# Work beside the second attention: dealt by two engines' budgets, with layernorm arithmetic moved from VectorE to GpSimd

## The chip, the cores and the metric

The kernel runs on one core of one Trainium2 chip. The core has five engines that run their own instruction queues side by side: TensorE (PE in the profile; its weight loads are PEld), VectorE (DVE), ScalarE (ACT), GpSimd (POOL) and SyncE (SP, which only issues DMAs). The metric is the device time of one execution in microseconds; lower is better. Before the change it is 1583.2 us, the median of three runs (1580.79 to 1584.08).

## The reference

The input is `x` of shape (4, 1024, 256) in f32. Four layers run one after the other, each as `x = x + layernorm(layer(layernorm(x)))`:

```
x = x + _layernorm(_L0_attn_ref(_layernorm(x), ...))   # grouped attention, groups of 64
x = x + _layernorm(_L0_ffn_ref(_layernorm(x), ...))    # low-rank feed-forward
x = x + _layernorm(_L1_attn_ref(_layernorm(x), ...))   # the second attention
x = x + _layernorm(_L1_ffn_ref(_layernorm(x), ...))    # 8 experts, each takes its top 1024 tokens
```

The change lies in the third. It has 16 heads of 16 dimensions over 1024 tokens, in each of 4 rows of the batch:

```
qkv = (x @ w_qkv).reshape(Bx, Sx, H, 3 * HD); q, k, v = split(qkv)
scores = einsum('bhqd,bhkd->bhqk', q, k) / sqrt(HD)
w = relu(scores);  attn = w / (sum(w, -1) + 1e-6)
out = einsum('bhqk,bhkd->bhqd', attn, v) @ w_out + b_out
y = x + out
return (y - mu) * rsqrt(var + eps) * gamma + beta
```

Here `x` is the layernormed input. The result is layernormed once more and added to the residual. The rows for the experts are the layernorm of that sum.

## The kernel before

Tokens are held as 8 tiles `xs[t]` of 512 tokens, each `[128, 4, 256]`. The two first layers run as one pipeline over these 8 tiles, then comes the second attention, then the experts.

**Blocks and steps.** The second attention loops over the 4 rows `b`, the 2 halves of queries `qh` of a row, the 4 groups of heads `g` and the 8 tiles of keys `kt`. I call one `(b, qh)` a block (numbered 0 to 7) and one `kt` a step: a block has 32 steps, a group 8. The last block goes through its queries in two halves of 256 with two key tiles a step, so that it has 32 steps too, and 4 steps a group. A step does the following.

- `scores` (L1388): TensorE makes the scores of 4 heads. Two go to PSUM tiles called `sc1`, two to a double tile `sc2`. ScalarE takes the relu of the first two into `w` (L1397, two instructions), VectorE that of the other two in one instruction of 1024 columns (L1402). In the last block, ScalarE takes that pair in every second step (L1400).
- `finish` of the step before (`weigh`, L1414): TensorE multiplies `w` by the values with a column of ones, accumulating over `kt` in one PSUM bank `po`. After the last `kt` of a group VectorE transposes `po` into `turned` (L1464), and the next group's first multiplication has to wait for that, since it writes the same bank.
- One piece of TensorE's side work from the list `beside`, and some of VectorE's and ScalarE's side work from the list `rest`.

Everything stands in each engine's queue in the order in which it is written (`manual_schedule` for PE, DVE and ACT); the queues of POOL and SP are ordered by the framework's scheduler. So an instruction that waits holds up whatever stands behind it on its engine. PSUM gives three buffers to the `sc1` tiles and TensorE's side pieces together, two to `sc2`; `w` has two buffers.

**Side work.** In blocks 0 to 5 the queries, keys and values of the next row are made, one half-row a block: `normalize` (layernorm of `xs`, statistics and `apply`), then `project`: two pieces that transpose `h` (`turn`, L392), two each for queries, keys (L400) and values (L433). Queries and keys are split into a high and a low part: ScalarE writes the high one (L408, L419), VectorE the low one (L409, L420), both into a tile `parts` with two buffers, and SP stores them to DRAM (`q_d`, `k_d`), from where GpSimd's queue fetches them for the next row (`fetch_queries` L377, `fetch_keys` L370). In blocks 1 to 7 the block before is closed (`close`): two pieces `project_out` (L1201), then for each of the 4 tiles of 128 tokens the chain `stats_y`, `affine`, statistics of that, `shift`, `add`, `stats_x`, `token_rows_and_on`; the last stores the rows for the experts, and appends TensorE's pieces for the gate (`tpg` L1265, `pg` L1280). `divide` normalizes the heads of two groups by their sums.

Statistics (`scale_of`) are `bn_stats`, `bn_aggr` and an addition of eps on VectorE, then `(var+eps)^-0.5` on GpSimd (L1116).

**Dealing.** `by_tile` lists a chain as all tiles' first step, then all tiles' second, and so on. `go_on` takes in each step one piece of `beside` and with it two of `rest`, without one it takes one of `rest`; after the last `kt` of a group it takes a piece of `beside` alone:

```
def go_on(room=1):
    if beside:
        beside.pop(0)()
        room *= 2
    for _ in range(room):
        if rest:
            rest.pop(0)()
```

The last block deals by a time for VectorE instead (`go_on_for`). After the last step what is left is done, then `at_once` closes the last two tiles by itself.

Of the kernel before, what the change touches and what calls it, by code (L numbers as in the profile page):

```python
# [14 lines left out]
ALU = mybir.AluOpType  # L15
# [59 lines left out]
def kernel(  # L75
# [146 lines left out]
    with ExitStack() as st1:  # L222
# [127 lines left out]

        def open_row(hs=None):

            row = {"h": hs or [act4("h") for _ in range(BPB)]}
# [736 lines left out]
    with ExitStack() as st3:  # L1090
# [16 lines left out]
        def scale_of(tag, src):  # L1107

            st = small.tile([P, 6], F32, tag=f"st{tag}", name=f"st{tag}")
            mv = small.tile([P, 2], F32, tag=f"mv{tag}", name=f"mv{tag}")  # L1110
            ve = small.tile([P, 1], F32, tag=f"ve{tag}", name=f"ve{tag}")
            rs = small.tile([P, 1], F32, tag=f"rs{tag}", name=f"rs{tag}")
            nc.vector.bn_stats(st, src)
            nc.vector.bn_aggr(mv, st)
            nc.vector.tensor_scalar(ve, mv[:, 1:2], EPS, None, ALU.add)  # L1115
            nc.gpsimd.tensor_tensor(rs, ve, mhalf[:, 0:1], ALU.pow)  # L1116
            return mv[:, 0:1], rs


        VECTOR_US = {"affine": 0.9, "shift": 0.43, "add": 0.42, "token_rows_and_on": 0.35}  # L1120

        def by_tile(*steps, tiles=range(NJ)):

            kept = {}

            def run(do, i):
                kept[i] = do(i, *kept.get(i, ())) or ()

            def piece(do, i):
                def go():  # L1130
                    run(do, i)

                go.us = VECTOR_US.get(do.__name__, 0.65)
                return go

            return [piece(do, i) for do in steps for i in tiles]

        def normalize(row, b, k):

            h, x = row["h"][k], xs[b * BPB + k]  # L1140

            def stats(i):
                return scale_of("a", x[:, i, :])

            def apply(i, mean, rs):
                nc.vector.tensor_scalar(h[:, i, :], x[:, i, :], mean, rs, ALU.subtract, ALU.mult)

            return by_tile(stats, apply)
# [20 lines left out]
        def divide(state, t):  # L1169
# [20 lines left out]

            by_weight.us, back.us = (0.7, 0.45) if n < TB else (1.3, 0.75)
            return [by_weight, back]

        def close(t, h, oT, tiles, at_end):
# [25 lines left out]

            def affine(i, mean, rs):
                nc.vector.scalar_tensor_tensor(y[:, i, :], y[:, i, :], mean, gam, ALU.subtract, ALU.mult)
                nc.vector.scalar_tensor_tensor(y[:, i, :], y[:, i, :], rs, bet, ALU.mult, ALU.add)

            def shift(i, mean, rs):
                ms = small.tile([P, 1], F32, tag="msc", name="msc")
                nc.vector.scalar_tensor_tensor(ms, mean, -1.0, rs, ALU.mult, ALU.mult)
                x = xs[t][:, i, :]
                nc.scalar.activation(x, x, AF.Identity, bias=ms)
                return (rs,)  # L1230
# [7 lines left out]

            def token_rows(i, mean, rs):
                if t < ADDED:  # L1240
                    nc.sync.dma_start(out_flat[t][:, i, :], xs[t][:, i, :])
                if i == tiles[0]:
                    gating["h"] = wk.tile([P, NJ, D], F32, tag="hg", name="hg")
                hg = gating["h"][:, i, :]
                nc.vector.tensor_scalar(hg, xs[t][:, i, :], mean, rs, ALU.subtract, ALU.mult)
                nc.sync.dma_start(tok_d[t * TB + i * P : t * TB + (i + 1) * P, 0:D], hg)
                if i == tiles[-1]:
                    js = slice(tiles[0], tiles[-1] + 1)
                    rows = x_d[t * TB : (t + 1) * TB, :].rearrange("(j p) d -> p j d", p=P)
                    nc.sync.dma_start(rows[:, js, :], xs[t][:, js, :])  # L1250

            def token_rows_and_on(i, mean, rs):
                token_rows(i, mean, rs)
                if i % 2:
# [52 lines left out]
            def at_once(by_weight, back):  # L1307
# [39 lines left out]
                for i, mean, rs in moments("g", x, "take"):  # L1347
                    token_rows(i, mean, rs)
                turn_gating(tiles[0])
# [26 lines left out]
        def scores(row, qh, q2, halves, g, kt):  # L1376
# [19 lines left out]
            for j, sc in enumerate(singles):  # L1396
                nc.scalar.activation(w[:, j, :], sc, AF.Relu)  # L1397
            if halves > 1 and kt // halves % 2:

# [26 lines left out]

        def go_on(room=1):
            if beside:
                beside.pop(0)()
                room *= 2  # L1430
            for _ in range(room):
                if rest:
                    rest.pop(0)()

        spare_time = [0.0]

        def go_on_for(us, weights_on_act):

            left = min(spare_time[0], 0.3) + us
            if beside:  # L1440
                beside.pop(0)()
                left -= 0.45
            while rest:

                takes = 0.8 if weights_on_act and rest[0].us == VECTOR_US["shift"] else rest[0].us
                if takes > left:
                    break
                left -= takes
                rest.pop(0)()
            spare_time[0] = left  # L1450

# [27 lines left out]
        for b in range(B):  # L1479
            after = open_row() if b + 1 < B else None  # L1480
            for qh in range(BPB):
# [3 lines left out]
                if after is not None:  # L1485
# [4 lines left out]

                    and_project.us = last.us
                    rest.extend((*steps, and_project))
                halves = 2 if (b, qh) == (B - 1, BPB - 1) else 1
                for q2 in range(halves):
                    for g in range(NG):
                        for kt in range(0, KT, halves):
                            w = scores(row, qh, q2, halves, g, kt)
                            if before is not None:
                                finish(*before)
                            if kt == halves and g % 2 == 0:  # L1500
# [5 lines left out]
                            at_end = kt == KT - halves  # L1506
                            if halves == 1:
                                go_on(0 if at_end else 1)
                            elif kt // halves % 2:
                                go_on_for(1.5 if at_end else 1.8, True)  # L1510
# [569 lines left out]
```

## Time and profile before

| | us |
|---|---|
| median of 3 runs | 1583.2 |
| the profiled execution | 1582.82 |
| its span | 1581.0 |
| second attention, first scores to the end of the last block | 419.5 to 1045 |
| experts after it, to the end | 1045 to 1581 |

Of the profiled execution 1.8 us lie outside the span. Busy shares over the span are TensorE 95%, VectorE 61%, ScalarE 41%, GpSimd 27%; these are means over four different stages. The mean granted TensorE clock is 0.979. A matmul's end is modelled in the trace, so that a busy TensorE can still be waiting: the starts of the instructions tell more than their lengths.

The starts of the scores give each block's time (from the timeline, first scores of a block to the first scores of the next; block 7 to the start of its last step):

| block | 0 | 1 | 2 | 3 | 4 | 5 | 6 | 7 (31 steps) |
|---|---|---|---|---|---|---|---|---|
| us | 80.4 | 79.7 | 79.1 | 83.3 | 79.3 | 81.7 | 66.5 | 71.3 |

### The profile page before, as it was taken

Reading aid. Unit: us, or ns where it says so; the run is one execution under the profiler, and the core shown is the slowest. Engines: PE = TensorE matmul, PEld = TensorE weight load, DVE = VectorE, ACT = ScalarE, POOL = GpSimd, SP = SyncE. Lnnn points to the kernel's source line nnn. Section 1 sums busy time; section 2 is a strip of 40 time slices with the busy share of each in tenths; the row PEclk is TensorE's granted clock in tenths of the full one; section 3 lists DMA queues with packets and bytes.
Section 4 is the critical chain, followed back from the end, with each engine's and each line's share of the span. In section 5 each row is a group of like instructions: output and inputs, shape, how many; then the busy total and the mean of one; then the engine's idle time right before and its main releaser. Section 6 shows DMA issues by size and latency. Waiting matters only on the chain. (4 is left out here: it accounts for less than half of the span.)

```text
span 1581.0 us, 24173 instructions
## 1 busy us (share of the span) xinstructions
PE 1498.6 (95%) x9286; PEld 797.3 (50%) x9286; DVE 966.5 (61%) x2266; ACT 642.8 (41%) x1117; POOL 425.5 (27%) x473
## 2 busy tenths in 40 slices
PE   8999999999699899999999999977999999999996
PEld 4666666666333333333323323534665666676674
DVE  5555665565457887878787897776463732222145
ACT  4344445543345454545454556752112112211232
POOL 4122323322210212021212111112424332342554
PEclk9999999999899999999999999988999999999998
DMA  8300000004322323223232401042224233243364
GB/s 212 123 1 1 0 1 1 1 1 149 118 90 71 107 95 108 94 85 117 94 101 74 135 28 55 28 122 70 68 50 101 64 72 74 49 96 70 71 155 125
DMA packets 91886, 121.59 MB, mean 77 GB/s; under 512 B 24925, under 2 KB 64250, under 8 KB 91642
## 3 DMA queue, kind: packets, MB, share of 16 engines
q1 hardware_dynamic: 70000, 73.09, 14.6%
q0 software_dynamic: 21712, 46.94, 12.9%
q8 instruction: 73, 1.20, 0.3%
q14 instruction: 43, 0.35, 0.1%
q10 hardware_dynamic: 58, 0.01, 0.0%
HBM read 66.90 MB, written 53.12 MB: 76 GB/s over the span
## 5 line engine op out<-in xcount | busy, mean ns | idle before, releaser
L1397 ACT ACTIVATE w<-sc 128x512 f32<-128x512 f32 x512 | 277.7, 595 | 166.5 <-ACT w L1397 63.2
L1402 DVE TENSOR_SCALAR w<-sc 128x1024 f32<-128x1024 f32 x240 | 292.8, 1220 | 52.6 <-PE sc L1388 32.2
L1414 PE MATMUL po<-w,vaug 128*17 128x512 f32 (+1 forms) x2304 | 301.9, 553 | 10.4 <-DVE turned L1464 8.5
L1955 PE MATMUL ph<-xT,w 128*128 128x512 f32 (+1 forms) x544 | 229.7, 575 | 0.3 <-DVE xT L1938 0.3
L1972 PE MATMUL py<-w,hid 128*128 128x256 f32 x1024 | 229.7, 381 | 0.0
L1962 ACT ACTIVATE hid<-ph,mb 128x512 f32<-128x512 f32 (+1 forms) x136 | 90.0, 662 | 340.0 <-PE ph L1955 249.6
L1972 PEld LDWEIGHTS py<-w,hid 128*128 128x128 f32 x1024 | 192.0, 190 | 31.4 <-issue 6.7
L1388 PE MATMUL sc<-q,kT 32*128 32x512 f32 (+1 forms) x2304 | 195.8, 416 | 9.9 <-ACT w L1397 8.5
L1388 PEld LDWEIGHTS sc<-q,kT 32*128 32x128 f32 x2304 | 88.6, 185 | 184.2 <-issue 157.3
L1955 PEld LDWEIGHTS ph<-xT,w 128*128 128x128 f32 x544 | 100.0, 190 | 106.9 <-issue 98.2
L1993 POOL DMA_INDIRECT acc_d<-y,idx x56 | 88.1, 1573 | 227.5 <-DVE y L1992 104.4
L1414 PEld LDWEIGHTS po<-w,vaug 128*17 128x17 f32 x2304 | 50.1, 96 | 127.1 <-issue 73.3
L1991 DVE TENSOR_TENSOR y<-py,mb 128x256 f32<-128x256 f32 x56 | 23.5, 419 | 126.3 <-PE py L1972 116.8
L1763 POOL DMA_INDIRECT got<-tok_d,idx x64 | 66.3, 1036 | 61.3 <-DVE counts L1597 24.4
L1938 DVE COPY xT<-tp 128x512 f32<-128x512 f32 (+1 forms) x34 | 22.2, 658 | 71.4 <-PE tp L1933 65.2
L716 PE MATMUL pg<-nT,wh 128*128 128x512 f32 x128 | 61.6, 614 | 1.5 <-ACT nT L655 1.4
L838 PE MATMUL py<-wo,oT 128*128 128x256 f32 x256 | 61.9, 385 | 0.0
L732 PE MATMUL pv<-wh,nT 128*128 128x512 f32 x128 | 59.7, 593 | 0.0
L1116 POOL TENSOR_TENSOR rsg<-veg,mhalf 128x1 f32<-128x1 f32 x30 | 16.7, 556 | 148.3 <-DVE veg L1115 148.3
L838 PEld LDWEIGHTS py<-wo,oT 128*128 128x128 f32 x256 | 47.3, 190 | 17.1 <-issue 9.6
L903 ACT ACTIVATE hid<-ph,vec 128x512 f32<-128x512 f32 x64 | 39.8, 685 | 27.3 <-PE ph L894 27.1
L588 POOL TENSOR_TENSOR x<-x,y 128x1024 f32<-128x1024 f32 x14 | 32.9, 2354 | 59.9 <-ACT y L577 59.8
(298 smaller groups left out, 1995.0 us busy)
## 6 DMA issues: line engine op xcount, KB each, us to landing
q<-q_d POOLq DMA_DIRECT2D x16, 1024.0 KB, 6.3
w<-in_L_ffn_W_dram SPq DMA_DIRECT2D x16, 1024.0 KB
q_d<-parts SPq DMA_DIRECT2D x48, 256.0 KB
kT<-k_d POOLq DMA_DIRECT2D x16, 512.0 KB, 6.0
k_d<-parts SPq DMA_DIRECT2D x24, 256.0 KB
acc_d<-logits SPq DMA_DIRECT2D x8, 512.0 KB
q_d<-wh SPq DMA_DIRECT2D x16, 256.0 KB
tok_d<-hg SPq DMA_DIRECT2D x32, 128.0 KB
```

Source lines behind the costliest of these rows:

```text
L716: nc.tensor.matmul(pg, lhsT=wh[:, c, HID + e * P : HID + (e + 1) * P], rhs=d["nT"][:, c, :], start=(c == 0), stop=(c == DC - 1),)
L732: nc.tensor.matmul(pv, lhsT=d["nT"][:, c, i * P : (i + 1) * P], rhs=wh[:, c, 0:HID], start=(c == 0), stop=(c == DC - 1),)
L838: nc.tensor.matmul(py, lhsT=d["oT"][:, e, :], rhs=wo[:, e, :], start=(e == 0), stop=(e == EC - 1))
L1388: nc.tensor.matmul(sc[:, m * n : (m + 1) * n], lhsT=row["kT"][t][rows, r, (kt + m) * P : (kt + m + 1) * P], rhs=row["q"][qh, t][rows, r, p ...
L1397: nc.scalar.activation(w[:, j, :], sc, AF.Relu)
L1402: nc.vector.tensor_scalar(w[:, 2:4, :], pair, 0.0, None, ALU.max)
L1414: nc.tensor.matmul(po[32 * j : 32 * j + HD + 1, weighed(halves, r)], lhsT=row["v"][:, kt + m, HQ * t + 4 * r + j, :], rhs=w[:, j, m * n : ...
L1763: return nc.gpsimd.indirect_dma_start(out=dst, out_offset=None, in_=rows[:, :], in_offset=self.at_chunk(c), bounds_check=NT - 1, oob_is_er ...
L1955: nc.tensor.matmul(ph, lhsT=w1[:, c, f * P : (f + 1) * P], rhs=xT[u][:, c, h * n : (h + 1) * n], start=(c == 0), stop=(c == DC - 1),)
L1962: nc.scalar.activation(hid[:, f, h * n : (h + 1) * n], ph, AF.Gelu, bias=mb1[:, e * FC + f : e * FC + f + 1])
L1972: nc.tensor.matmul(py, lhsT=hid[:, f, i * P : (i + 1) * P], rhs=w2[:, f, :], start=(f == 0), stop=(f == FC - 1),)
L1993: scatter = nc.gpsimd.indirect_dma_start(out=acc_d[:, :], out_offset=lists[e].at_chunk(k), in_=y, in_offset=None, bounds_check=NT - 1, oob ...
```

## The change

The change does six things, all in the second attention.

1. `scale_of` also makes `ms = -mean * rs` on GpSimd, one instruction of one column behind the power. `shift` loses its own instruction on VectorE for that.
2. Three kinds of VectorE work become GpSimd work: `apply` (the layernormed `h`), `affine` (two instructions on VectorE; three on GpSimd: scale and shift, times gamma, plus beta), and the layernormed rows `hg` in `token_rows_and_on`. The closing of the last two tiles, `at_once`, keeps them on VectorE.
3. `by_tile` staggers a chain: the n-th step of tile i gets the place 2.5 n + i.
4. TensorE's pieces of `beside` are taken in odd steps alone; in the first step of a group (step 1) the piece stands between the scores and the multiplication by the values, in the others after it.
5. Pieces of `rest` carry two numbers, VectorE's and ScalarE's microseconds. Each step adds to a budget of both; pieces are taken as long as both budgets cover the next one. A piece of TensorE adds 1.2 to both.
6. ScalarE takes the pair's relu in every fourth step of the last two blocks (8 in each), where it had every second step of the last block (16).

```diff
+            ms = small.tile([P, 1], F32, tag=f"ms{tag}", name=f"ms{tag}")
             nc.gpsimd.tensor_tensor(rs, ve, mhalf[:, 0:1], ALU.pow)
-            return mv[:, 0:1], rs
-        VECTOR_US = {"affine": 0.9, "shift": 0.43, "add": 0.42, "token_rows_and_on": 0.35}
+            nc.gpsimd.tensor_scalar(ms, mv[:, 0:1], rs, -1.0, ALU.mult, ALU.mult)
+            return rs, ms
+
+        def scaled(dst, src, rs, ms):
+            nc.gpsimd.tensor_scalar(dst, src, rs, ms, ALU.mult, ALU.add)
+
+        NEITHER, STATS = (0.2, 0.2), (0.76, 0.0)
+        TAKES = {
+            "affine": NEITHER, "shift": (0.0, 0.6), "add": (0.48, 0.0), "token_rows_and_on": NEITHER,
+            "apply": NEITHER,
+        }
...
-            return [piece(do, i) for do in steps for i in tiles]
+            order = sorted((2.5 * n + i, do, i) for n, do in enumerate(steps) for i in tiles)
+            return [piece(do, i) for _, do, i in order]
...
-            def apply(i, mean, rs):
-                nc.vector.tensor_scalar(h[:, i, :], x[:, i, :], mean, rs, ALU.subtract, ALU.mult)
+            def apply(i, rs, ms):
+                scaled(h[:, i, :], x[:, i, :], rs, ms)
...
-            by_weight.us, back.us = (0.7, 0.45) if n < TB else (1.3, 0.75)
+            by_weight.takes, back.takes = ((0.9, 0.0), (0.45, 0.0)) if n < TB else ((1.2, 0.0), (0.65, 0.0))
...
-            def affine(i, mean, rs):
-                nc.vector.scalar_tensor_tensor(y[:, i, :], y[:, i, :], mean, gam, ALU.subtract, ALU.mult)
-                nc.vector.scalar_tensor_tensor(y[:, i, :], y[:, i, :], rs, bet, ALU.mult, ALU.add)
-            def shift(i, mean, rs):
-                ms = small.tile([P, 1], F32, tag="msc", name="msc")
-                nc.vector.scalar_tensor_tensor(ms, mean, -1.0, rs, ALU.mult, ALU.mult)
+            def affine(i, rs, ms):
+                scaled(y[:, i, :], y[:, i, :], rs, ms)
+                nc.gpsimd.tensor_tensor(y[:, i, :], y[:, i, :], gam, ALU.mult)
+                nc.gpsimd.tensor_tensor(y[:, i, :], y[:, i, :], bet, ALU.add)
+            def shift(i, rs, ms):
                 x = xs[t][:, i, :]
                 nc.scalar.activation(x, x, AF.Identity, bias=ms)
                 return (rs,)
...
-                nc.vector.tensor_scalar(hg, xs[t][:, i, :], mean, rs, ALU.subtract, ALU.mult)
+                hg_of(hg, xs[t][:, i, :])
...
+            def token_rows_and_on(i, rs, ms):
+                token_rows(i, lambda dst, src: scaled(dst, src, rs, ms))
...
-            if halves > 1 and kt // halves % 2:
+            if row["last"] and kt // halves % 4 == 2:
                 nc.scalar.activation(w[:, 2:4, :], pair, AF.Relu)
...
-        def go_on(room=1):
+        room = [0.0, 0.0]
+        def next_piece():
             if beside:
                 beside.pop(0)()
-                room *= 2
-            for _ in range(room):
-                if rest:
-                    rest.pop(0)()
+                for i in range(2):
+                    room[i] += 1.2
+        def go_on(vector, scalar):
+            for i, more in enumerate((vector, scalar)):
+                room[i] = min(room[i], 1.2) + more
+            while rest and all(need <= left for need, left in zip(rest[0].takes, room)):
+                go = rest.pop(0)
+                for i in range(2):
+                    room[i] -= go.takes[i]
+                go()
...
                             w = scores(row, qh, q2, halves, g, kt)
+                            step, at_end = kt // halves, kt == KT - halves
+                            if step == 1:
+                                next_piece()
                             if before is not None:
                                 finish(*before)
...
+                            if step % 2 and step > 1:
+                                next_piece()
+                            vector = 0.4 - (0.65 / halves if at_end else 0.0)
+                            if row["last"] and step % 4 == 2:
+                                go_on(vector + 1.2, -0.6)
                             else:
-                                go_on_for(0.9, False)
+                                go_on(vector, 0.4)
...
         while beside or rest:
-            go_on()
+            next_piece()
+            go_on(1.0, 1.0)
```

More of the change, by code (lines that the diff above doesn't have):

```diff
@@ L347, with open_row @@
             )
-        def open_row(hs=None):
-            row = {"h": hs or [act4("h") for _ in range(BPB)]}
+        def open_row(hs=None, last=False):
+            row = {"h": hs or [act4("h") for _ in range(BPB)], "last": last}
             row["q"], row["kT"] = {}, {}
@@ L1131, in go @@
                     run(do, i)
-                go.us = VECTOR_US.get(do.__name__, 0.65)
+                go.takes = TAKES.get(do.__name__, STATS)
                 return go
-            return [piece(do, i) for do in steps for i in tiles]
+            order = sorted((2.5 * n + i, do, i) for n, do in enumerate(steps) for i in tiles)
+            return [piece(do, i) for _, do, i in order]
         def normalize(row, b, k):
@@ L1237, in stats_x, with token_rows @@
                 return scale_of("g", xs[t][:, i, :])
-            def token_rows(i, mean, rs):
+            def token_rows(i, hg_of):
                 if t < ADDED:
@@ L1250, in token_rows @@
                     nc.sync.dma_start(rows[:, js, :], xs[t][:, js, :])
-            def token_rows_and_on(i, mean, rs):
-                token_rows(i, mean, rs)
+            def token_rows_and_on(i, rs, ms):
+                token_rows(i, lambda dst, src: scaled(dst, src, rs, ms))
                 if i % 2:
@@ L1347, in at_once @@
                 for i, mean, rs in moments("g", x, "take"):
-                    token_rows(i, mean, rs)
+                    token_rows(
+                        i,
+                        lambda dst, src, mean=mean, rs=rs: nc.vector.tensor_scalar(
+                            dst, src, mean, rs, ALU.subtract, ALU.mult
+                        ),
+                    )
                 turn_gating(tiles[0])
@@ L1425 @@
         beside, rest = [], []
-        def go_on(room=1):
+        room = [0.0, 0.0]
+        def next_piece():
             if beside:
                 beside.pop(0)()
-                room *= 2
-            for _ in range(room):
-                if rest:
-                    rest.pop(0)()
[L1435 to L1450, printed above, removed]
+                for i in range(2):
[8 more added lines that the diff above has]
+                go()
         state = {}
@@ L1479 @@
         for b in range(B):
-            after = open_row() if b + 1 < B else None
+            after = open_row(last=b + 2 == B) if b + 1 < B else None
             for qh in range(BPB):
@@ L1489, in and_project @@
                         beside.extend(project(*to))
-                    and_project.us = last.us
+                    and_project.takes = last.takes
                     rest.extend((*steps, and_project))
@@ L1497 @@
                             w = scores(row, qh, q2, halves, g, kt)
+                            step, at_end = kt // halves, kt == KT - halves
+                            if step == 1:
+                                next_piece()
                             if before is not None:
                                 finish(*before)
-                            if kt == halves and g % 2 == 0:
+                            if step == 1 and g % 2 == 0:
                                 if g == 0 and q2 == 0:
@@ L1504 @@
                                     fetch_queries(*((row, 1) if qh == 0 else (after, 0)), 0)
[L1506 to L1510, printed above, removed]
+                            if step % 2 and step > 1:
[3 more added lines that the diff above has]
+                                go_on(vector + 1.2, -0.6)
                             else:
-                                go_on_for(0.9, False)
+                                go_on(vector, 0.4)
                             before = (row, b, qh, q2, halves, g, kt, w)
```

## The prediction

> **What bounds the kernel now.** I read the page first (busy shares), then the timeline of TensorE through the second attention, the table of waits for 419.5 to 1045 us, the windows of single blocks, and the durations by form of the instructions that the change touches.
>
> The page says that TensorE is nearly always busy:
>
> ```profile
> PE 1498.6 (95%) x9286; PEld 797.3 (50%) x9286; DVE 966.5 (61%) x2266; ACT 642.8 (41%) x1117; POOL 425.5 (27%) x473
> ```
>
> Matmul ends are modelled, so I take the starts instead. In the timeline a step runs from its scores to the next scores:
>
> ```profile
> 609.12 0.74 PE L1388 MATMUL sc<-q,kT 32*128 32x512 f32 x8
> 609.79 1.05 PE L1414 MATMUL po<-w,vaug 128*17 128x512 f32 x8
> ...
> 610.78 1.99 PE L400 MATMUL pk<-hT,wk 128*128 128x512 f32 x4
> 612.69 0.74 PE L1388 MATMUL sc<-q,kT 32*128 32x512 f32 x8
> 613.36 1.37 PE L1414 MATMUL po<-w,vaug 128*17 128x512 f32 x8
> 616.27 1.98 PE L400 MATMUL pk<-hT,wk 128*128 128x512 f32 x4 [1.54 <-DVE parts L420]
> 618.19 0.74 PE L1388 MATMUL sc<-q,kT 32*128 32x512 f32 x8
> ```
>
> The first step takes 612.69 - 609.12 = 3.57 us and loses nothing: scores 0.67, values 0.98, piece 1.92. The second has the same contents and takes 5.50. Sorted so, the shortest step with only scores and values takes 1.65 us; a transposing piece (`tp`, `tpg`) adds 0.59, a projecting one (`pq`, `pk`, `pv`, `pt`) 1.92, the gate `pg` 0.85. The 255 steps of the stage take 621.2 us, their contents by these prices 540.6. So 80.6 us is waiting, 8 to 15 us a block, and the contents don't change. The waits name it:
>
> ```profile
> ACT parts L419 <- DMA q_d<-parts: 43.6, 11, 4.7
> PEld po L1414 <- DVE turned L1464: 17.3, 21, 1.6
> PEld pk L400 <- DVE parts L420: 16.6, 6, 3.2
> PEld po L1414 <- DVE w L1402: 16.0, 28, 1.2
> ```
>
> ScalarE's `parts` waits for a store, since the tile has two buffers; TensorE's next piece then waits for the PSUM tile that `parts` should have read. Sorting the 80.6 by what is late: steps with keys or values behind that store 25.2; plain steps and first `po` behind VectorE 28.4; first steps of a group behind `turned` 12.65; start of block 0 9.5; other pieces 4.6.
>
> VectorE has little slack within a block (columns: us, each engine's busy us and groups, clock, DMA share, GB/s):
>
> ```profile
> 570.00:648.00 78.00, 74.28 (x572) 25.18 (x568) 64.88 (x118) 40.75 (x76) 13.65 (x23) 1.00 0.29 95
> 648.00:727.00 79.00, 74.75 (x560) 26.05 (x560) 64.06 (x121) 39.98 (x75) 14.46 (x24) 0.98 0.32 103
> ```
>
> VectorE 64.88 of 78 us, GpSimd 13.65: the mean leaves room on both, the order decides.
>
> **What the Trainium skill says.** "GPSIMD Engine Reference", section 3.1 (elementwise cycle accounting), gives 2.6 cycles an element for two inputs and 1.8 for the best one-input loop, 769 ns for 512 elements. The trace agrees:
>
> ```profile
> L364 POOL TENSOR_TENSOR h<-h,b1o x32: 717/726/997, 351.2 to 851.2; 128x256 f32<-128x256 f32 x32
> L673 POOL TENSOR_SCALAR head<-qk,vec x16: 762/982/1236, 16.9 to 312.7; 128x512 f32<-128x512 f32 x16
> L1116 POOL TENSOR_TENSOR rsb<-veb,mhalf x30: 542/548/655, 524.4 to 1021.2; 128x1 f32<-128x1 f32 x30
> L1402 DVE TENSOR_SCALAR w<-sc x240: 1183/1224/1226, 428.2 to 1039.0; 128x1024 f32<-128x1024 f32 x120
> ```
>
> (shortest/median/longest ns.) "SBUF — State Buffer", section "SBUF: two separate sides", says that GpSimd and VectorE share a port pair as an exclusive lock, for VectorE's fast modes and for its instructions with two SBUF inputs. Before this stage the trace shows it: one VectorE instruction of 128x4 takes 158 to 1693 ns, a two-input one of 128x256 451 to 957. In this stage it doesn't: the relu reads PSUM and takes 1.224 at the median and 1.226 at most, whether GpSimd runs or not.
>
> **The change part by part.**
>
> *VectorE to GpSimd.* Per closed block VectorE loses four `affine` (0.475 + 0.484), four `msc` (0.149), four `hg` (0.405), and in blocks 0 to 5 four `apply` (0.40): 3.84 + 0.60 + 1.62 + 1.60 = 7.7 us of some 64. GpSimd gains per tile three `ms`, a scale and two tensor_tensor of 0.726, an `hg`, an `apply`. The new `scaled` is 128x256 with one tensor input. Not in the trace of before; from below it is half the page's 769 ns (0.38), from above the whole 0.62 (half of 1.236); I take 0.5, half the median row. `ms` is at least the 0.198 of a 128x4 multiply and at most the power's 0.55; I take 0.3 with the gap. A block gets about 12 x 0.3 + 4 x (0.5 + 1.45 + 0.5 + 0.5) = 15.4, rising to 17 with gaps, on top of 13.65: 31 of 75 us. Throughput holds. Latency: an affine tile is 0.55 + 0.31 + 0.55 + 0.81 + 0.81 = 3.0 us instead of 0.55 + 0.96 = 1.5.
>
> *Odd steps.* Before, two 3.57 steps follow the queries, so the store that the keys' `parts` needs, landing about 8.5 us after its low part is written, is late by 7.13. With pieces in every second step, 2 x 3.57 + 2 x 1.65 = 10.44 us pass. The store is in time: of the 25.2 nothing is left (0 to 6 for a store that is itself issued later behind SP's other DMAs). Placing the piece of step 1 ahead of `po` also covers `turned` there, 0.48 a group. Where `beside` is empty at step 1 it does not: eleven groups at 0.48, blocks 6, 2 and 4 in the second group 1.2 + 0.64 + 0.64, block 7 four at 0.3: 9.0, instead of 12.65.
>
> *VectorE by budget.* A piece at a step's end is followed by the next step's `po`, 2.8 us after the scores that feed it. The relu (1.22) plus the evacuation `y = pt + h` (0.69) leave 0.7 for other work, `parts` (ScalarE 0.60, then VectorE 0.69) leave none. Following the written order through the blocks I find late relus: odd blocks 0.6 + 0.67, even ones 0.8 + 0.4 + 0.67 + 1.4, plain steps with statistics (0.67 + 1.22 = 1.89 against 1.65) 0.3 a block: 11.7, instead of 28.4 and 4.6.
>
> *New waits, in order.* `shift` on ScalarE now waits for GpSimd's `ms`, and the relus of later steps are queued behind it; TensorE waits for those. In blocks 1, 3 and 5 `fetch_keys`, whose DMAs are issued on GpSimd's queue and wait for `k_d` to land (about 6.5 us after the keys' piece), stands between the power and `ms` of one tile: about 2.0 us each. In blocks 2 and 4 the `ms` of the first tile stands behind an affine chain and the additions to `h`, some 2.85 us late: 1.2 + 0.65 each. Block 6 with eight pairs moved to ScalarE (1.03 each against budgets of -0.6): 8 x 0.15 + 2 x 0.5 = 2.2. Block 7: 8 x 0.25 + 0.5 + 1.8 = 4.3, where ScalarE is close to its limit anyway:
>
> ```profile
> 962.00:1045.00 83.00, 79.84 (x1157) 41.19 (x1154) 61.04 (x143) 59.25 (x101) 11.43 (x20) 1.00 0.13 40
> ```
>
> Together 6.0 + 3.7 + 2.2 + 4.3 = 16.2 us, new.
>
> *Tail.* The last `stats_x`, `hg`, its transposes, gate and logits of the second last group come to stand after the last `turned`, ahead of the last `divide`: +4.8, less 1.5 that leaves the loop: +3.3. On SP the rows' store moves with `hg`; it is read only by the experts, more than a block later for all but the last tiles.
>
> *Sum.* Start 9.5, stores 0, groups 9.0, VectorE 11.7, in order 16.2 = 46.4 against 80.6; with the tail -34.2 + 3.3 = -30.9. The same walk over block 2 of the kernel before gives 6.3 us of waiting where 8.3 are measured, that is three quarters; so I scale what I walked, 36.9, to 48.6. That takes 11.7 back: -30.9 + 11.7 = -19.2. From the profiled 1582.82 this gives 1563.6; its distance to the median of the runs (1583.2) is 0.4, too small to carry. I say 1563.
>
> **The rivals.**
>
> *The gain is larger.* The in-order waits (16.2 and their share of scaling) could be absorbed, as `w` has two buffers and a late `shift` costs only what exceeds a step's slack. For it: ScalarE is busy 40.75 of 78 us. Against: half a step is all that two buffers give. If half of the scaled waiting (48.6) goes: 1563 - 24 = about 1541.
>
> *The gain is given back.* VectorE's order in the even blocks, where statistics of two chains meet, costs nearly as much as before (28.4 + 4.6 = 33.0 where the scaled sum has 11.7 / 0.76 = 15.4): 1563 + 17.6 = about 1581, no change. Against: 7.7 us less work a block.
>
> *Slower: GpSimd's chain is the bound.* If a tile's chain takes over some 4.5 us instead of 3.0 (one-input forms near 1 us as the longest L673 row, and GpSimd waiting for the port pair behind two-input VectorE instructions), four tiles no longer fit between statistics dealt at 2.5 places and one step, and every `ms` is late in order behind the affine chain of the tile before. ScalarE's `shift` then holds up relus: 1.5 us a tile at 4 tiles and in 2 chains, less 3 of slack, is 9 in the even blocks 0 to 6, 5 to 6 in the odd ones: about 4 x 9 + 3 x 5.5 = 52, of which 16 is in the sum already. With half a block's more at the tail: 1563 + 28 to 36, so 1591 to 1599; I take 1593. It decides above 4 us a tile. For it: the trace shows POOL forms that vary by 1.6 times. Against: the additions to `h` at 726 median never pass 997 in this very stage.
>
> *The change doesn't do what it says.* Budgets too tight could leave work over until after the last step. The order as built leaves only the last tile's end (the tail above), so I give this no share of its own.
>
> **How the numbers follow.** Forecast 1563, own range 1551 to 1575 (stores 0 to 6 more, `scaled` 0.38 to 0.62, scaling none or twice: about -12, +12): 0.55. Larger gain, about 1541: 0.18. Given back, about 1581 (half of it within the bound): 0.11. GpSimd as the bound, 1593: 0.16. To leave no more than 2 in 10 out, the range takes the forecast's, the upper half of the larger gain and the given-back case: 1540 to 1585. About 3 us, 0.2%, is what a measurement of this kernel can tell from no change: faster 0.55 + 0.18 + 0.05 = 0.78, within 0.05, slower 0.16 + 0.01 = 0.17.
>
> **What would show it.** Right: the wait of `parts` (L419 before) for `q_d` falls from 43.6 to under 5 us; the wait of `po` for `turned` from 17.3 to about 9; blocks 0 to 5 take 74 to 79 us each where they took 79 to 83; GpSimd's busy time in a block is near 31 us and VectorE's near 57; the new `scaled` takes 0.4 to 0.62 and `ms` 0.2 to 0.3. A new wait of ScalarE's `x` for GpSimd's `msc` of 10 to 20 us shows the price of part 1. Wrong: `scaled` near 1 us or VectorE's two-input instructions (statistics no, `x` add of 0.474 and `y`) stretched beside GpSimd; a wait of TensorE for `w` of either engine above 30 us; block times in alternation by over 8 us between even and odd; or a stage after 1045 us that differs by over 2 us, since nothing there is touched.

## The result and the profile after

The changed kernel takes 1592.5 us (median of 4 runs, 1590.8 to 1592.66) beside 1582.55 for the kernel before: a ratio of 1.0061, with a 95% interval from 1.0043 to 1.0078. It is slower by some 10 us where I had forecast 20 less.

Where they lie is read from four landmarks of each trace: the first scores, the end of the last `turned`, the first comparison of the experts (`ge`), and the end. I call the stretch between the first two the loop, and that between the second and third the close. In us:

| | first scores at | loop | close | from there to the end | span |
|---|---|---|---|---|---|
| before | 419.5 | 625.7 | 15.9 | 519.9 | 1581.0 |
| after | 420.7 | 627.3 | 21.9 | 519.2 | 1589.0 |

So the experts are untouched, the close is 6.0 longer, and the loop, where I had expected to gain 22, is 1.5 longer. The moved work went where it should. The page's busy times (us, and shares of the span) are:

```profile
PE 1507.4 (95%) x9286; PEld 797.6 (50%) x9286; DVE 920.8 (58%) x2122; ACT 643.5 (40%) x1117; POOL 547.2 (34%) x731
```

VectorE has lost 45.7 us and GpSimd gained 121.7. TensorE's waiting over the 255 steps, by the same prices of a step's contents as before, is 83.4 us, where it was 80.6:

| block | 0 | 1 | 2 | 3 | 4 | 5 | 6 | 7 |
|---|---|---|---|---|---|---|---|---|
| us, after | 75.8 | 83.7 | 80.8 | 83.1 | 80.2 | 83.3 | 66.1 | 70.3 |
| of it waiting, before | 14.9 | 9.2 | 8.3 | 11.4 | 8.5 | 9.7 | 7.8 | 10.9 |
| of it waiting, after | 10.3 | 13.8 | 8.0 | 13.2 | 7.4 | 13.4 | 6.8 | 10.5 |

The three odd blocks stand out. The timeline of TensorE in block 1 after the change, steps 20 to 24, shows one place:

```profile
544.70 0.74 PE L1402 MATMUL sc<-q,kT 32*128 32x512 f32 x8
545.37 1.05 PE L1428 MATMUL po<-w,vaug 128*17 128x512 f32 x8
546.35 0.74 PE L1402 MATMUL sc<-q,kT 32*128 32x512 f32 x8
547.02 2.07 PE L1428 MATMUL po<-w,vaug 128*17 128x512 f32 x8
549.02 1.98 PE L400 MATMUL pk<-hT,wk 128*128 128x512 f32 x4
550.93 0.74 PE L1402 MATMUL sc<-q,kT 32*128 32x512 f32 x8
551.60 1.05 PE L1428 MATMUL po<-w,vaug 128*17 128x512 f32 x8
554.32 0.50 PE L1402 MATMUL sc<-q,kT 32*128 32x512 f32 x1 [1.66 <-DVE parts L420]
558.04 1.22 PE L1402 MATMUL sc<-q,kT 32*128 32x512 f32 x7 [3.23 <-ACT w L1411]
559.20 1.91 PE L1428 MATMUL po<-w,vaug 128*17 128x512 f32 x8
561.04 2.99 PE L433 MATMUL pv<-wv,hT 128*128 128x256 f32 x8
563.95 0.74 PE L1402 MATMUL sc<-q,kT 32*128 32x512 f32 x8
```

Step 22 takes 3.38 us for 1.65 of contents, step 23 9.63 for 3.57: 7.8 us lost in two steps. In blocks 3 and 5 the same two steps lose 7.2 and 7.4, so that it is 22.5 over the three. What TensorE waits for stands in ScalarE's timeline of the same time:

```profile
552.94 0.60 ACT L419 ACTIVATE parts<-pk 128x512 fp32r<-128x512 f32 x1 [4.69 <-DMA q_d<-parts]
553.44 0.50 ACT L1238 ACTIVATE x<-x,msc 128x256 f32<-128x256 f32 x1
557.00 0.51 ACT L1238 ACTIVATE x<-x,msc 128x256 f32<-128x256 f32 x1 [3.06 <-POOL msc L1118]
557.41 1.07 ACT L1411 ACTIVATE w<-sc 128x512 f32<-128x512 f32 x2
```

Two waits, one after the other, with the relus of the next scores queued behind the second. And GpSimd's timeline says why `msc` is late:

```profile
539.21 0.78 POOL L377 DMA_DIRECT2D q<-q_d  x1
...
548.82 0.55 POOL L1117 TENSOR_TENSOR rsc<-vec,mhalf 128x1 f32<-128x1 f32 x1 [0.94 <-DVE vec L1115]
555.87 0.78 POOL L370 DMA_DIRECT2D kT<-k_d  x1 [6.50 <-DMA k_d<-parts]
556.70 0.27 POOL L1118 TENSOR_SCALAR msc<-mvc,rsc 128x1 f32<-128x1 f32 x1
```

Between a tile's power (548.82) and its `ms` (556.70) stands the fetch of the keys, which waits 6.50 us for their store. And the 1 MB fetch of queries goes out at 539.21, in the middle of the stores of the second piece of queries; before the change, with a start of the stage that is 1.1 us earlier, it went out at 548.40, when these were done. From the end of a low part to the landing of its store, where `parts` waited for it, 11.0 to 13.6 us pass in the four waits after the change; in the eleven before it was 7.8 to 9.9. The table of waits of 419.5 to 1060 us, the lines that answer to those of before and two new ones:

```profile
PEld sc L1402 <- ACT w L1411: 57.8, 51, 8.8
PEld po L1428 <- DVE w L1416: 24.0, 38, 1.4
ACT x L1238 <- POOL msc L1118: 16.4, 7, 3.4
ACT parts L419 <- DMA q_d<-parts: 16.0, 4, 4.7
PEld po L1428 <- DVE turned L1472: 15.2, 23, 1.5
```

The stores' wait fell from 43.6 to 16.0, and others grew: the weight loads of the values wait longer for VectorE's relu (16.0 before) although VectorE has less to do, and those of the scores for ScalarE's relu, 17.3 us in 17 places before, wait 57.8 in 51. A weight load can wait while TensorE still multiplies, so these are no sums of lost time: in the kernel that is 37 us faster (below) the wait for ScalarE's relu is still 47.2. The wait of the scores' multiplication itself for that relu went from 8.5 us in 2 places to 20.5 in 6.

### The profile page after: what moved, and what is told of

The parts are those of the page before. It is cut to its first block, busy times and chain, and to the rows that moved or that the text cites. A ratio compares the mean times of both kernels' runs of the same rounds, so it can differ in the third digit from the quotient of the medians.

```text
span 1589.0 us, 24205 instructions
## 1 busy us (share of the span) xinstructions
PE 1507.4 (95%) x9286; PEld 797.6 (50%) x9286; DVE 920.8 (58%) x2122; ACT 643.5 (40%) x1117; POOL 547.2 (34%) x731
## 3 DMA queue, kind: packets, MB, share of 16 engines
q0 software_dynamic: 21712, 46.94, 13.1%
## 5 line engine op out<-in xcount | busy, mean ns | idle before, releaser
L1428 PE MATMUL po<-w,vaug 128*17 128x512 f32 (+1 forms) x2304 | 311.2, 558 | 8.0 <-DVE turned L1472 6.0
L1402 PE MATMUL sc<-q,kT 32*128 32x512 f32 (+1 forms) x2304 | 195.7, 417 | 26.2 <-ACT w L1411 20.5
L838 PEld LDWEIGHTS py<-wo,oT 128*128 128x128 f32 x256 | 47.2, 190 | 17.1 <-issue 9.6
L810 PE MATMUL po<-packed,v 128*128 128x128 f32 x256 | 48.9, 280 | 0.0
```

What stands on the lines that cost most here:

```text
L838: nc.tensor.matmul(py, lhsT=d["oT"][:, e, :], rhs=wo[:, e, :], start=(e == 0), stop=(e == EC - 1))
L1402: nc.tensor.matmul(sc[:, m * n : (m + 1) * n], lhsT=row["kT"][t][rows, r, (kt + m) * P : (kt + m + 1) * P], rhs=row["q"][qh, t][rows, r, p ...
L1428: nc.tensor.matmul(po[32 * j : 32 * j + HD + 1, weighed(halves, r)], lhsT=row["v"][:, kt + m, HQ * t + 4 * r + j, :], rhs=w[:, j, m * n : ...
```

## The experiments

Four theories were at stake. **Q**: GpSimd's queue, where the fetch of the keys stands ahead of `ms`. **D**: the DMAs, where the fetch of queries slows the stores. **G**: GpSimd's arithmetic is too slow as a chain, the rival that I had priced at 1593. **O**: the order of dealing around a piece of TensorE makes VectorE's relu late. The ratio is to runs of the kernel before that were made beside those of each kernel. The landmarks are in the table at the end of the section.

**GpSimd in the written order**, from the changed kernel:

```diff
-        st3.enter_context(tc.manual_schedule(engines={engines.PE, engines.DVE, engines.Activation}))
+        st3.enter_context(tc.manual_schedule(engines={engines.PE, engines.DVE, engines.Activation, engines.Pool}))
```

> The changed kernel with GpSimd's queue in the written order too, so that the keys' fetches stand behind the values' pieces and no longer between one tile's power and its ms. Theory Q (GpSimd's queue: the fetch of the keys, waiting for its store, holds up ms, that holds up ScalarE's shift and the relus behind it): steps 22 and 23 of blocks 1, 3 and 5, which lose 1.7 + 6.1 us each now, lose under 3 together; 1592.5 - 15 = about 1577. Theory D (the 1 MB fetch of queries beside the stores makes these land late): the wait of ScalarE's parts for q_d (16.0 us in 4 waits) stays, TensorE still loses over 5 us at steps 22 and 23: 1586 to 1592. Theory G (GpSimd's arithmetic is too slow as a chain): no change, 1589 to 1595.

1586.1 us, ratio 1.0024 (1.0017 to 1.0031): 6.4 less than the changed kernel. Steps 22 and 23 of block 1 lose 1.40 + 1.94 us instead of 1.73 + 6.06, and over blocks 1, 3 and 5 they lose 10.4 instead of 22.5. So Q holds for these 12 us. About half of them is lost again elsewhere: blocks 0, 2 and 7 wait 2.0, 1.2 and 2.7 us longer, and the close is 1.5 longer. The time is at the lower edge of D's band and 9 us above Q's, and the wait of `parts` for `q_d` stays, as D said:

```profile
ACT parts L419 <- DMA q_d<-parts: 16.2, 4, 4.4
```

The edit orders all of GpSimd's queue, not the fetches alone, so that a part of these gains and losses can have another source.

**The queries' fetch at step 25**, on top of that:

```diff
-                            if step == 1 and g % 2 == 0:
+                            if step == 1 and g in (0, 3):
```

> The kernel with GpSimd in written order, and the 1 MB fetch of queries at step 25 of a block instead of step 17, away from the stores of queries and keys. Theory D: the waits of ScalarE's parts for q_d fall from 16.0 us to under 4, and the time is 5 to 15 us below that of the run with the written order alone. Theory Q: under 3 us from that run. Theory G: the same as that run.

1576.4 us, ratio 0.9962 (0.9948 to 0.9976): 9.7 less again, as D expected, and faster than before the change. In its table of waits there is no wait of `parts` for `q_d` any more, where the stores of the run above landed 12.1 to 13.1 us after their low parts; in block 1 step 22 loses nothing and step 23 1.77. In the profiled executions 5.1 of the 9.7 us lie in these two steps of the odd blocks and 1.4 in block 2; another 3.3 lie in blocks 0 and 7, where no wait for a store stood, and what brought those isn't shown. The two edits together were worth 16 us, the whole of the loss and more. I call this kernel the one with both cures.

**Odd steps alone**, on the kernel before (blocks 0 to 6; what a piece's step takes from `rest` stays as it was):

```diff
-        def go_on(room=1):
-            if beside:
+        def go_on(room=1, piece=True):
+            if beside and piece:
...
-                                go_on(0 if at_end else 1)
+                                go_on(0 if at_end else 1 + early, step % 2 == 1 and step > 1)
```

(`early` is true where the piece of step 1 was taken between scores and values.)

> The kernel before with one part of the change alone: TensorE's pieces in odd steps in blocks 0 to 6. My forecast's term: the stores' stalls (25.2 us) go, 1582.5 - 20 = about 1563 to 1570. Theory D: the stores land late in the odd blocks beside the fetch of queries, so that half of the 25 stays: 1570 to 1576. Theory Q: the power behind the fetch of the keys holds up the shift here too, 4 to 7 us in each of three blocks, which eats the rest: 1580 to 1586.

1598.5 us, ratio 1.0096 (1.0079 to 1.0113): slower than any of the three expected. It isn't the stores: their wait is down from 43.6 to 6.6 us. It is this line, 16.0 us before:

```profile
PEld po L1414 <- DVE w L1402: 49.3, 56, 2.2
```

My reading, which no run tests alone: a piece that is followed by a short step leaves VectorE less time than a row of pieces does, and it still gets two statistics in that step. Besides, every second step isn't enough to take all pieces in: the close is 24.3 us instead of 15.9.

**VectorE's work back on VectorE**, in the changed kernel (its budget 0.6 a step instead of 0.4):

```diff
-            nc.gpsimd.tensor_scalar(dst, src, rs, ms, ALU.mult, ALU.add)
+            nc.vector.tensor_scalar(dst, src, mean, rs, ALU.subtract, ALU.mult)
...
-                nc.gpsimd.tensor_tensor(y[:, i, :], y[:, i, :], gam, ALU.mult)
-                nc.gpsimd.tensor_tensor(y[:, i, :], y[:, i, :], bet, ALU.add)
+                nc.vector.scalar_tensor_tensor(y[:, i, :], y[:, i, :], mean, gam, ALU.subtract, ALU.mult)
+                nc.vector.scalar_tensor_tensor(y[:, i, :], y[:, i, :], rs, bet, ALU.mult, ALU.add)
```

> The changed kernel with apply, affine, the rows and the product for the shift on VectorE again (budget of VectorE 0.6 a step instead of 0.4, their own takes): the other parts stay. Theory G: GpSimd's chain is the loss, so 1568 to 1576. Theory Q: the power for the shift still stands behind the fetch of the keys, the loss at steps 22 and 23 of odd blocks stays over 4 us, and VectorE's 7.7 us a block come back in part: 1588 to 1600. The tail after the last step, 8 us longer now, becomes shorter by 3 to 5 in any theory, since rows and power chain are shorter.

1601.95 us, ratio 1.0124 (1.0107 to 1.0141). G falls: without GpSimd's arithmetic it is 9.5 us slower. But Q's reason for that wasn't right either: steps 22 and 23 lose at most 0.4 us in blocks 1 and 3, and the 4.0 of step 23 in block 5 come with ScalarE's `shift` waiting 2.3 for VectorE's own `msc`, not for a fetch. The loss is spread over many pieces, and the weight loads of the values wait 51.4 us for VectorE's relu. The close is 16.4, 5.5 less than after the change, as expected of shorter chains.

The same edit **on the kernel with both cures** takes out what Q and D mix in:

> The kernel with GpSimd in written order and the queries' fetch at step 25 (1576.4), with apply, affine, the rows and the product for the shift on VectorE (budget 0.6 a step). If VectorE's amount of work is what GpSimd relieves, the loop grows by 10 to 25 us, the end shortens by 5 to 7 since the rows are made at once: 1582 to 1596. If GpSimd's chains hold up more than they relieve: 1560 to 1572.

1603.7 us, ratio 1.0136 (1.0119 to 1.0153), 27 above that kernel, more than I had expected: its loop is 34 us longer, its close 7.3 shorter. Of the parts that are taken back here, the move of the arithmetic to GpSimd costs most when it goes. The edit changes VectorE's budget and prices with it, and no run separates the two.

**Another end**, on the kernel with both cures: the last tile's statistics and rows ahead of the last transposition, the gate's pieces inside the closing of the last tiles:

```diff
-        finish(*before)
-        while beside or rest:
-            next_piece()
-            go_on(1.0, 1.0)
-        state["close"][0](*divide(state, DC - 1))
+        while rest:
+            rest.pop(0)()
+        finish(*before)
+        state["close"][0](*divide(state, DC - 1), *beside)
```

(`at_once` runs what it is given behind its first statistics, and reads the gate's result after its affine part.)

> The kernel with GpSimd in written order and the queries' fetch at step 25, with another end: the statistics of the last tile and its rows stand ahead of the last transposition of the sums, and the gate's two pieces stand inside the closing of the last two tiles, beside its statistics, instead of ahead of the last division. If the pieces left over are what makes the end 8 us longer after the change, the time falls by 5 to 8 us from that kernel's 1576.4, to 1568.5 to 1571.5. If the end is bound by something else (the shift's wait in the last two steps), by under 2.

1570.35 us, ratio 0.9922 (0.9906 to 0.9939): 6.1 less, within the band. The close falls from 23.7 to 18.0.

**Dealing ahead of the piece** tests O:

```diff
-                            if step % 2 and step > 1:
-                                next_piece()
+                            piece = step % 2 and step > 1 and beside
+                            if piece:
+                                for i in range(2):
+                                    room[i] += 1.2
...
+                            if piece:
+                                beside.pop(0)()
```

On the kernel with both cures alone:

> The dealing ahead of TensorE's piece alone, on the kernel with GpSimd in written order and the queries' fetch at step 25 (1576.4), the end unchanged: if the order is what matters, 1552 to 1562; if the amount, 1574 to 1578.

1568.8 us, ratio 0.9916 (0.9900 to 0.9933): 7.7 less, half of the least that O expected, but clearly not nothing. Blocks 1, 3 and 5 wait 4.2 to 5.0 us instead of 7.5 to 7.7, and the line of O falls from 30.7 to

```profile
PEld po L1428 <- DVE w L1416: 17.2, 37, 1.9
```

In blocks 2 and 4 it gains 0.1 and 1.7 only, since something else comes up. With the other end as well:

> The kernel of the first run of this set with one more edit: in an odd step the pieces of VectorE and ScalarE are dealt ahead of TensorE's piece, not behind it, so that they fill the time in which VectorE waits for that piece's result. If VectorE's late relus are due to this order (1 to 2 us at each of pq, pk, pv and pt, some 5 us a block in blocks 1 to 5), the loop gains 15 to 25 us more: 1545 to 1556. If they are due to the amount of VectorE's work, nothing: within 3 us of the first run.

1563.3 us, ratio 0.9877 (0.9859 to 0.9895), 7.1 below the kernel with the other end alone: the two gains add up, but the second is again about half of the least expected.

**What came up in blocks 2 and 4** is again GpSimd's queue. In the timeline of the dealing alone, on GpSimd:

```profile
608.59 0.55 POOL L1117 TENSOR_TENSOR rsc<-vec,mhalf 128x1 f32<-128x1 f32 x1
609.25 0.26 POOL L1118 TENSOR_SCALAR msc<-mvc,rsc 128x1 f32<-128x1 f32 x1
609.48 0.55 POOL L1122 TENSOR_SCALAR y<-y,rsb,msb 128x256 f32<-128x256 f32 x1
610.12 0.72 POOL L1233 TENSOR_TENSOR y<-y,gam 128x256 f32<-128x256 f32 x1
610.92 0.73 POOL L1234 TENSOR_TENSOR y<-y,bet 128x256 f32<-128x256 f32 x1
611.62 0.54 POOL L1117 TENSOR_TENSOR rsc<-vec,mhalf 128x1 f32<-128x1 f32 x1
612.26 0.26 POOL L1118 TENSOR_SCALAR msc<-mvc,rsc 128x1 f32<-128x1 f32 x1
```

and on ScalarE:

```profile
612.55 0.51 ACT L1238 ACTIVATE x<-x,msc 128x256 f32<-128x256 f32 x1 [1.53 <-POOL msc L1118]
613.42 0.51 ACT L1238 ACTIVATE x<-x,msc 128x256 f32<-128x256 f32 x1 [0.36 <-POOL msc L1118]
613.84 0.56 ACT L408 CAST parts<-pq 128x512 fp32r<-128x512 f32 x1
```

and on TensorE:

```profile
615.18 1.04 PE L1402 MATMUL sc<-q,kT 32*128 32x512 f32 x8 [2.39 <-DVE parts L409]
```

Four additions of the bias to `h`, 0.74 us each, stood ahead of these and pushed the chain back; `parts` stands behind the shifts, and TensorE's next scores wait 2.39 us for the bank that it reads. Moved behind the last piece of the values:

```diff
-            steps = row_steps(row, k, side, new_hT, new_parts)
+            steps = row_steps(row, k, side, new_hT, new_parts, with_bias=False)
...
+                        if (name, z) == ("values", 1):
+                            add_bias(row, k)
```

> The kernel with the other end and the dealing ahead of TensorE's piece (1563.3), with the four additions of the bias to h (0.74 us each on GpSimd) behind the last piece of the values instead of behind the second transposing piece. In its blocks 2 and 4 these stand on GpSimd between one tile's affine and the next tile's ms, and step 15 to 17 lose 2.6 + 1.6 us each. If GpSimd's queue is the cause there, these fall under 1.5 together and the time to 1556 to 1560; if not, 1562 to 1565.

1555.8 us, ratio 0.9826 (0.9810 to 0.9842), at the lower end of the expected band and the fastest of all: 26 us under the kernel before, 37 under the changed one. Blocks 2 and 4 wait 4.1 and 3.3 us instead of 8.6 and 7.7. Its windows of blocks 1 and 2 and of block 7 (columns as before):

```profile
498.90:573.10 74.20, 73.00 (x576) 24.56 (x572) 60.90 (x103) 41.89 (x78) 32.02 (x62) 1.00 0.32 104
573.20:650.00 76.80, 76.00 (x596) 26.03 (x596) 60.32 (x103) 42.69 (x79) 30.43 (x60) 1.00 0.33 107
940.20:1014.20 74.00, 67.72 (x1044) 36.44 (x1048) 52.97 (x109) 45.75 (x81) 27.95 (x56) 0.97 0.10 33
```

Beside them block 2 of the changed kernel:

```profile
580.30:661.00 80.70, 78.58 (x597) 26.43 (x596) 60.13 (x103) 42.96 (x80) 31.29 (x61) 1.00 0.32 99
```

The busy times are nearly the same; what differs is the order.

**Pieces in every step again**, on the kernel with both cures:

```diff
-                            if step == 1:
-                                next_piece()
...
-                            if step % 2 and step > 1:
-                                next_piece()
+                            next_piece()
```

> The kernel with GpSimd in written order and the queries' fetch at step 25, with TensorE's pieces taken in every step again, behind the multiplication by the values, as before the change. My forecast's term: the stores' stalls return, 1576.4 + 15 to 25 = 1591 to 1601. If odd steps cost more than they bring (late relus behind each piece), it becomes faster: 1562 to 1574.

1588.2 us, ratio 1.0038 (1.0030 to 1.0047): 11.8 slower, somewhat under the band. The stores' wait is back:

```profile
ACT parts L419 <- DMA q_d<-parts: 45.6, 11, 8.5
```

But most of it costs TensorE little: blocks 1 to 5 wait 40.3 us together, where they wait 38.3 with pieces in odd steps. The loss is in block 0, which waits 21.3 us instead of 10.4, 8.3 of it in one step. There the store that the first keys waited for landed 12.3 us after its low part, again beside a fetch of queries: in block 0 GpSimd has little in its queue and issues the fetch of step 25 already at 461.04, in step 15. This fits D once more. That taking pieces in odd steps brings something by itself no run shows; on the kernel before it cost 16 us.

**The chains not staggered**, on the same kernel:

```diff
-            order = sorted((2.5 * n + i, do, i) for n, do in enumerate(steps) for i in tiles)
-            return [piece(do, i) for _, do, i in order]
+            return [piece(do, i) for do in steps for i in tiles]
```

> The same kernel (1576.4) with the chains listed as before the change, all tiles' first step, then all tiles' second. If the stagger hides GpSimd's latency (3 us a tile): slower, 1580 to 1590, with more waits of ScalarE's shift for ms. If it only brings the chains' tiles out of step: within 2 us.

1585.5 us, ratio 1.0023 (1.0015 to 1.0031): 9.1 slower, in the band. But the reason that I gave doesn't show: ScalarE's shift waits 6.7 us for `ms`, less than the 10.4 of the staggered one. The loop is 9.3 us longer, 5.2 of it waiting in the steps (block 6 waits 10.1 us instead of 6.8) and 4.1 behind the last scores; the cause these runs don't settle.

**The pairs as before the change**, on the same kernel, in the last block's odd steps, with the budgets of +1.2 and -0.6 there:

```diff
-            if row["last"] and kt // halves % 4 == 2:
+            if halves > 1 and kt // halves % 2:
...
-                            if row["last"] and step % 4 == 2:
+                            if halves > 1 and step % 2:
```

> The same kernel (1576.4) with the pair's relu on ScalarE in every second step of the last block alone, as before the change, its budgets moved to the same steps. My forecast's terms for the new placing were 2.2 us in block 6 and 4.3 in block 7; if they are its price: 1570 to 1574. If eight pairs in each of two blocks relieve VectorE as much as sixteen in one: 1575 to 1578. If better: 1579 to 1584.

1594.4 us, ratio 1.0075 (1.0058 to 1.0092), but this doesn't measure the placing: the loop is 610.0 us, as without the edit (611.0), and the close 42.4 instead of 23.7. With -0.6 in every second step ScalarE's budget no longer covers the shifts, so that chains are left over at the end. What the placing alone is worth stays open.

| | median us | loop | close |
|---|---|---|---|
| GpSimd in written order | 1586.1 | 621.7 | 23.4 |
| and the fetch at step 25 (both cures) | 1576.4 | 611.0 | 23.7 |
| and the other end | 1570.4 | 611.7 | 18.0 |
| and the dealing ahead of the piece, without the other end | 1568.8 | 602.2 | 23.8 |
| both | 1563.3 | 603.7 | 18.0 |
| and the bias later | 1555.8 | 597.6 | 18.1 |
| both cures, arithmetic on VectorE | 1603.7 | 645.0 | 16.4 |
| both cures, pieces in every step | 1588.2 | 626.8 | 17.9 |
| both cures, not staggered | 1585.5 | 620.3 | 23.8 |
| both cures, pairs as before | 1594.4 | 610.0 | 42.4 |
| before, with odd steps alone | 1598.5 | 634.2 | 24.3 |
| after, arithmetic on VectorE | 1602.0 | 643.9 | 16.4 |

## Why the prediction was wrong

The direction was wrong. My sum had 9.5 + 48.6 = 58.1 us of waiting in the loop and 3.3 more at the end; measured are 83.4 and 6.0. The steps that failed are the store's landing, which I took to be independent of what else the DMAs carry, and what a fetch in GpSimd's queue does to the `ms` behind it. By the sum's own steps:

- **The arithmetic on GpSimd** was priced right. `scaled` takes 0.55 us where I took 0.5, `ms` 0.26 (0.3 with its gap), the chain of an affine tile 3.2 at the shortest from the power to its last instruction (3.0), with other work between 3.8 at the median and 4.5 at most. GpSimd's busy time in block 2 is 31.3 us (31). Taking it back, with the budgets that go with it, costs 27 us.
- **Stores** ("of the 25.2 nothing is left, 0 to 6"): failed. 16.0 us of ScalarE's wait are left. I set the landing at about 8.5 us against a gap of 10.44 (the "late by 7.13" of the text is the time that two such steps take, not a delay), from a trace in which the 1 MB fetch of queries ran after the stores. Beside the fetch the landing took 11.0 to 13.6. The fetch is written in step 17, where it was; queries and keys, in steps 11 to 14 of block 1 before, now stand in 15 to 21, on either side of it. I had walked SP's stores and not asked what else moves data then. Moving the fetch brought 9.7 us.
- **The odd blocks** ("about 2.0 us each"): the mechanism was named, GpSimd's fetch of the keys between power and `ms`; the size was about a quarter of the 7.2 to 7.8 measured. Two terms were wrong: the first keys' store let GpSimd go 11 us after their piece had ended (544.8 to 555.9), not 6.5, beside the same fetch; and the late `parts` and the late `ms` come one after the other on ScalarE, so that their delays add. This is 22.5 us against my 6.0, or 7.9 scaled: 14.6 of the 25.3 that the loop's sum missed.
- **VectorE by budget** (11.7 instead of 33): failed in sign for the wait for the relu itself, which grew from 16.0 to 24.0. Blocks 1 to 5 without steps 22 and 23 of the odd ones wait 33.3 us, where my terms for them (groups 5.1, VectorE 11.7, in order 3.7) make 20.5, or 27 scaled. I had the limit, 2.8 us from the scores to the multiplication that needs the relu, and mis-sized what stands in it: the pieces of `rest` are dealt behind TensorE's piece, at the moment when both budgets have just been raised by 1.2, so they go right in front of the next relu. The dealing ahead of the piece brought 7.7 us. Moving the four additions to `h`, which I had among the waits in order, brought 7.5.
- **Groups** (wait for `turned` from 17.3 to about 9): 15.2 is left.
- **Blocks 6 and 7**: 17.3 us of waiting, where my terms (6.5 in order, 3.4 for groups) make 9.9, or 13.0 scaled. Why stays open.
- **The end** (+3.3): named right, 6.0 measured. The other end took 5.7 of 23.7.
- **The experts** stayed within 0.7 us, as I had said.

Of the **rivals**, "GpSimd's chain is the bound" gave 1593 and comes within a microsecond, which is luck: its mechanism isn't what happened. The chain takes 3.8 us a tile at the median, under the 4 from which I had said that it decides and over it in 4 of 30 tiles, and taking it away makes things worse. What it had right is where the damage comes out: ScalarE's `shift`, in order ahead of the relus, waiting for GpSimd. The main cause was what else stood in GpSimd's queue, a fetch that waits for a DMA, and not GpSimd's speed. "The gain is larger" assumed that a late `shift` would be absorbed by the two buffers of `w`; the 12 us that steps 22 and 23 gained in the odd blocks once no fetch stood ahead of `ms` say otherwise.

A gain like the forecast's came only with edits that it doesn't contain: GpSimd's written order, the later fetch, the other end, the dealing ahead of the piece and the later bias, together 1555.8 us. So that time doesn't confirm the sum; it shows that the work as moved leaves room for such a gain. What I left out was that what stands in GpSimd's queue, and what the DMAs carry at the same time, changed with the rest without being written anywhere in the diff.

## What to carry to other kernels

When a wait is to go because work is moved later, look for every transfer that stays where it was and now runs beside it. A small result that an in-order engine waits for should not stand in a queue behind a DMA that waits for a landing; write that queue's order out too, or put the DMA behind. And try filler work ahead of the instruction that makes an engine wait: behind it, it can delay the next item on the path, here by 7.7 us in all.

## What the runs showed of the hardware

The Trainium skill describes a port pair that GpSimd and VectorE share as an exclusive lock ("SBUF — State Buffer", "SBUF: two separate sides"). Although GpSimd is busy 31 of 80 us in a block, the medians show nothing of it. VectorE's addition to `x`, which reads two tensors in SBUF, kept its 0.476 us:

```profile
L1243 DVE SCALAR_TENSOR_TENSOR x<-y,rsc,x x30: 442/476/506, 556.8 to 1040.5; 128x256 f32<-128x256 f32 x30
```

and `scaled` hardly varied on GpSimd, from 544 to 558 ns:

```profile
L1122 POOL TENSOR_SCALAR y<-y,rsb,msb x30: 544/552/558, 525.9 to 1034.2; 128x256 f32<-128x256 f32 x30
```

Single instructions show waits that fit such a lock. Of the 114 powers in the stage after the change, seven ran beside that addition, and these seven took 715 to 762 ns; the others took 543 to 574. In the kernel with the bias later, three of VectorE's additions to `x` started while GpSimd was adding the bias to `h`, which reads two tensors as well. They took 725 to 730 ns, and the addition to `h` behind each of them 917 to 922 instead of some 730. In the changed kernel the seven powers make some 1.3 us of GpSimd's time in all, far less than the change lost.

The 552 ns of `scaled` are some 45% above the 0.38 us that I had worked out from the one-input loop of the Trainium skill ("GPSIMD Engine Reference", section 3.1) for 256 elements. Already in the trace before, only the shortest 128x512 row of GpSimd (762 ns) agreed with the 769 of that section; the median was 982. The measured time decides.
